# Value projection of 14 head groups by seven half-size products instead of eight (Strassen's scheme), with the last output product between its steps

## The chip, the cores and the metric

The kernel runs on one core of a Trainium2 chip. The core has five engines with queues of their own: TensorE (PE, matrix products, with a separate row PEld for its weight loads), VectorE (DVE), ScalarE (ACT), GpSimd (POOL) and SyncE (SP, which here only issues DMA). Each engine works its queue strictly in the order in which the program was written; between engines there are only semaphores. The metric is the time of one execution on the device in microseconds (us).

## The reference, cut to what matters

Two layers over `x` of shape 8 x 512 x 256, all in float32. Each layer normalises its input and adds an attention part and a feed-forward part to it. The change lies in the attention of the first layer, which has 16 heads of 64:

```
xn = layernorm(x)
q, k, v = xn @ Wq + bq, xn @ Wk + bk, xn @ Wv + bv        # each 256 -> 1024
q, k = rope(q), rope(k)
attended = softmax(causal(q k^T / 8)) @ v
x = x + attended @ Wo + bo + int8_product(xn)
```

The second layer (comparison attention and a gated feed-forward part) is not touched.

## The kernel before, in words

The work of layer 1 is cut into 16 groups, numbered `at` = 0 to 15. Group `at` is batch `b = at // 2` and half `g = at % 2` of the heads: eight heads, 512 of the 1024 columns of q, k and v. For each group the kernel does these steps:

- `project_qk` (line 428): queries and keys of the group, matrix products of 512 columns into PSUM, kept by ACT, and a rotated copy `y` fetched by DMA. `project(at, which)` calls it for both quarters of a group. `turn_qk` multiplies by the rotation's tables on DVE (line 446) and adds on POOL (line 461).
- `project_v` (line 472): the values of the group. For each of four tiles of 128 tokens, two accumulating products with 512 columns of `Wv` (the two halves of the 256 inputs), so eight products. ACT copies each bank to SBUF (line 478), and SP stores the result `v` to DRAM (line 479), from where `load_v` fetches it back rearranged as `vr` (line 489).
- `scores(at, run)` (line 509): query block times keys, in five runs that cover the 16 query blocks of 32 rows; run 3 is blocks 9, 5, 8 and 6, run 4 is block 7.
- `soften(at, run)`: DVE adds the mask and finds the maximum (line 537), ACT exponentiates and sums (line 541). `divide(at, run)`: DVE takes the reciprocal (line 552), POOL scales (line 560). `turn(at, run)`: DVE transposes 32 x 32 blocks into the tiles `t_0` to `t_3` (line 580).
- `weigh(at)` (line 597): chances times values into four banks. `keep_weighed`: ACT adds the bias (line 611).
- `output_product(at, half)` (line 390): attended times `Wo`, per half eight products of 256 columns. `add_output` (line 399): DVE adds it to the running output `x1`. `finish(at)` calls both for both halves.

The order is written out by hand in the loop `for at in range(1, last)` with `last = 15`; no scheduler moves anything. One iteration stands like this (DVE, ACT and POOL parts in brackets, in the order of their queues):

```
scores(at, 0)   [turn(at-1, 4); soften(at, 0)]
weigh(at-1)     [keep_weighed; turn_qk for the keys of at+1; divide(at, 0)]
scores(at, 1)   [soften; turn(at, 0); in some iterations look_at; divide(at, 1)]
project(at+1, 0)
scores(at, 2)   [soften; turn_qk for the queries of at+1; turn(at, 1); divide(at, 2);
                 prepare or turn_x of a later batch in some iterations]
project_v(at+1)
scores(at, 3)   [soften; turn_qk; turn(at, 2); divide(at, 3)]
scores(at, 4)   [soften]
                (at = 12 and 13: add_quantised)
finish(at-1)    [add_output x 2]
                [turn(at, 3)]
project(at+2, 1)
                [divide(at, 4); add_biases when g = 0]
```

`look_at` (statistics of a later batch's input) comes when g = 1, and `prepare` (normalising and its greatest value) too; `turn_x` comes when g = 0. Iteration `at = 1` also loads the constants of the rest, and on POOL it adds the biases to batch 0's output. Iteration `at = 14` leaves the loop after `project_v`; a tail written out by hand follows. PSUM has eight banks, which all these steps share.

Of the kernel before, what the change touches and what calls it, by code (L numbers as in the profile page):

```python
# [8 lines left out]
F32 = mybir.dt.float32  # L9
# [3 lines left out]
ALU = mybir.AluOpType  # L13
# [3 lines left out]
P = 128  # L17
B, S, D = 8, 512, 256
H, L = 16, 64
NT = S // P  # L20
NK = D // P
# [9 lines left out]
NH = NP // 4  # L31
# [13 lines left out]
def two_layers(  # L45
    ctx: ExitStack, tc, x, turns, Wq, Wk, Wv, Wo, w8, rows, sides, second, gates, out,
):
    nc = tc.nc
# [11 lines left out]
    def bank(name):  # L60
        return ps.tile([P, S], F32, tag="b", name=name)
# [23 lines left out]
    wqkv = [const.tile([P, NG, NK, 4 * L], F32, name=f"w{n}") for n in "qkv"]  # L85
# [49 lines left out]
    def load_second():  # L135
        nc.scalar.dma_start(crl, sides.rearrange("(k p) n -> p k n", p=P))
        nc.scalar.dma_start(gs, gates)
# [122 lines left out]
    with ExitStack() as c0:  # L260
        c0.enter_context(tc.manual_schedule())

        def pool(name, bufs, **kw):
            return c0.enter_context(tc.tile_pool(name=name, bufs=bufs, **kw))

        work = pool("work", 1)
# [3 lines left out]
        away = pool("away", 2, space=bass.MemoryType.DRAM)  # L270
# [20 lines left out]
        xnT = {}  # L291
# [71 lines left out]
        def scale_of_x():  # L363
            pb = bank("pmax")
            nc.tensor.transpose(pb[:, :P], spread.pop(0), ident)
            g = small.tile([P, 1], F32, tag="g", name="g", bufs=1)
            nc.vector.tensor_reduce(g, pb[:, :P], AX.X, ALU.max)
            nc.vector.tensor_scalar(xs[:, 0:1], g, 1.0 / 127.0, Q_EPS, ALU.mult, ALU.max)
            nc.vector.reciprocal(xs[:, 1:2], xs[:, 0:1])
# [4 lines left out]
        def fetch(b):  # L374
            x1s[b] = output_tile(f"x1_{b}")
            nc.sync.dma_start(x1s[b], tokens(b))
# [4 lines left out]

        products = {}

        def output_product(at, half):

            pw = bank(f"pw_{at}_{half}").rearrange("p (j n) -> p j n", j=2)
            for j in range(2):
                tok = bass.ts(2 * half + j, P)
                for p in range(4):
                    nc.tensor.matmul(  # L390
                        pw[:, j, :], atts[at, p][:, tok], wo[:, 4 * (at % NH) + p, :],
                        start=(p == 0), stop=(p == 3),
                    )
            products[at, half] = pw

        def add_output(at, half):
            b, g = divmod(at, NH)
            rows = slice(2 * half, 2 * half + 2)
            nc.vector.tensor_tensor(  # L399
                x1s[b][:, rows, :], products.pop((at, half)), x1s[b][:, rows, :], ALU.add  # L400
            )

            if g == NH - 1 and half == 1 and b < B - 1:
                nc.sync.dma_start(x1_far[b], x1s[b].rearrange("p t n -> p (t n)"))

        def finish(at):
            for half in range(2):
                output_product(at, half)
                add_output(at, half)
# [3 lines left out]
        evicted, stores = {}, {}  # L413
# [25 lines left out]
        def turn_qk(at, which):  # L439

            turn_own(at, which)
            turn_other(at, which)
# [20 lines left out]
        def project_v(at, halves=(0, 1)):  # L463
            b, g = divmod(at, NH)
            if 0 in halves:
                stores[at] = away.tile([4, P, NT * P], F32, tag="v", name=f"va_{at}")
            for half in halves:
                v = work.tile([P, 4, 2, P], F32, tag="v", name=f"v_{at}_{half}", bufs=2)
                for j in range(2):
                    pb = bank(f"pv_{at}_{half}_{j}")  # L470
                    for k in range(NK):
                        nc.tensor.matmul(  # L472
                            pb.rearrange("p (g n) -> p g n", g=2),
                            xnT[b][:, k, 2 * half + j],
                            wqkv[2][:, 2 * g : 2 * g + 2, k, :],
                            start=(k == 0), stop=(k == NK - 1),
                        )
                    nc.scalar.copy(v[:, :, j, :], pb.rearrange("p (r n) -> p r n", r=4))
                nc.sync.dma_start(
                    stores[at][:, :, half * 2 * P : half * 2 * P + 2 * P].rearrange("r p n -> p r n"),  # L480
                    v.rearrange("p r t n -> p r (t n)"),
                )

        def load_v(at):

            there = stores.pop(at)
            vs[at] = work.tile([P, 4, NT, P], F32, tag="vr", name=f"vr_{at}")
            for j in range(4):
                nc.sync.dma_start(
                    vs[at][j * Q : j * Q + Q].rearrange("p c t n -> p c (t n)"),  # L490
                    there[j].rearrange("(c k) n -> k c n", c=4),
                )
# [93 lines left out]
        half = S // Q // 2  # L586
# [192 lines left out]
        def project(at, which):  # L779
            for half in range(2):  # L780
                project_qk(2 * at + half, which)
# [60 lines left out]
        for at in range(1, last):  # L842
            b, g = divmod(at, NH)
            two = at + 2 <= last
            if g == 0 and b < B - 1:
                fetch(b)
            scores(at, 0)
            turn(at - 1, 4)
            soften(at, 0)
            if at == last - 3:  # L850
                scale_of_x()
            weigh(at - 1)
            keep_weighed(at - 1)
            if at == 1:
                load_rest()
                load_second()
                fetch(0)
            turn_qk(2 * at + 2, 1)
            load_v(at)
            if at in (last - 3, last - 2):  # L860
                s_ = at - last + 3
                fetch_output(s_, output_tile(f"x1e_{s_}"))
                xnl = fetch_input(s_, work.tile([P, NK * S], F32, tag="xnl", name=f"xnl_{s_}"))
            divide(at, 0)
            turn_qk(2 * at + 3, 1)
            if at == last - 2:
                first_norm = norm(0, xpool.tile([P, NT, D], F32, tag="x", name="yn_0"))
            scores(at, 1)
            soften(at, 1)
            turn(at, 0)  # L870
            if at == 2:
                look_at(2)
            elif at == 4:
                spread_rest()
                spread_second()
            elif g == 1 and 1 <= b < B - 2:
                look_at(b + 2)
            divide(at, 1)
            if at == last - 1:
                first_norm()  # L880
            project(at + 1, 0)
            if at in (last - 3, last - 2):
                round_input(xnl)
            scores(at, 2)
            soften(at, 2)
            turn_qk(2 * at + 2, 0)
            turn(at, 1)
            if at in (last - 3, last - 2):
                xq = work.tile([P, NK * S], BF16, tag="xq", name=f"xq_{s_}")
                clip(xnl, xq)  # L890
            divide(at, 2)
            if at == 2:
                prepare(2)
            elif g == 1 and 1 <= b < B - 2:
                prepare(b + 2)
            if g == 0 and 1 < b < B - 1:
                turn_x(b + 1)
                if b + 2 < B:
                    x_next.append(load_x(b + 2))
            if at == last - 1:  # L900
                turn_qk(2 * at + 3, 0)
            if at == 1:
                nc.gpsimd.tensor_tensor(bob, bob, rw[:, 2, :], ALU.add)
                add_biases(0)
            project_v(at + 1)
            if at == last - 1:
                break
            if at == 2:
                transpose_x(2)
                x_next.append(load_x(3))  # L910
            scores(at, 3)
            soften(at, 3)
            turn_qk(2 * at + 3, 0)
            turn(at, 2)
            divide(at, 3)
            scores(at, 4)
            soften(at, 4)
            if at in (last - 3, last - 2):
                for half in range(2):
                    add_quantised(s_, half, xq, line(f"u_{s_}_{half}"))  # L920
            finish(at - 1)
            turn(at, 3)
            if two:
                project(at + 2, 1)
            divide(at, 4)
            if g == 0 and b < B - 1:
                add_biases(b)
            if at == last - 4:
                greatest()


        at = last
# [52 lines left out]
        r = gate(0)  # L985
# [13 lines left out]
        for b in range(B):  # L999
# [18 lines left out]
            else:  # L1018
                r = gate(b)
# [17 lines left out]
            y = work.tile([P, NT, D], F32, tag="v", name=f"y_{b}", bufs=2)  # L1037
# [72 lines left out]
```

## Time and profile before

| | |
|---|---|
| median of 3 runs | 935.68 us (935.48 to 936.91) |
| span of the profiled execution | 934.3 us |
| PE busy | 919.8 us |
| DVE busy | 793.3 us |
| POOL busy | 542.2 us |
| ACT busy | 528.3 us |
| mean granted TensorE clock | 1.000 |

The profiled execution is one execution of its own; its own time is its span, from the first to the last instruction, 1.4 us under the median of the runs.

In the groups of the page, one program product in float32 appears as several records on PE (256 for the 128 products of `project_v`), so a cost is best taken from the timeline: where one group of instructions starts and where the next one does. A timeline row gives the start, the length, the engine and line, the operation, the output and input tiles with the shape of the first one, the count, and in brackets the idle time of the engine before it and what ended that.

### The profile page before, as it was taken

How to read it: one execution, taken by the hardware profiler on the slowest of the kernel's cores; microseconds unless marked ns; L12 is line 12 of the kernel's file. 1: busy time of each engine (PE TensorE's matmuls, PEld its weight loads, DVE VectorE, ACT ScalarE, POOL GpSimd, SP SyncE). 2: the span in 40 equal slices, each digit the busy share in tenths (PEclk: the TensorE clock that was granted, in tenths of full speed). 3: DMA queues.
4: the chain of work that ended last, by engine and by line, in shares of the span. 5: the costliest groups of instructions: out<-in, count | busy, mean ns of one | idle time of the engine just before them, and what ended most of it. 6: DMA issues, size and time to landing. Idle time of an engine off the chain costs nothing.

```text
span 934.3 us, 27432 instructions
## 1 busy us (share of the span) xinstructions
PE 919.8 (98%) x10451; PEld 594.7 (64%) x10451; DVE 793.3 (85%) x2441; ACT 528.3 (57%) x1478; POOL 542.2 (58%) x688
## 2 busy tenths in 40 slices
PE   9998999999999999999999999999999999999998
PEld 5446565656566575757565656566657777777776
DVE  4998898898899889988998899999899588888854
ACT  3585564647465646474746556555577444445553
POOL 2576766655665667566665756678667323444311
PEclk9999999999999999999999999999999999999999
DMA  7667354525543464245444635563435133221011
GB/s 213 194 165 213 102 138 130 121 75 132 169 105 97 109 182 132 75 115 172 123 95 114 179 93 145 151 154 97 110 108 127 47 102 79 74 50 48 25 33 34
DMA packets 70290, 108.03 MB, mean 116 GB/s; under 512 B 8592, under 2 KB 49040, under 8 KB 70160
## 3 DMA queue, kind: packets, MB, share of 16 engines
q1 hardware_dynamic: 68288, 104.64, 42.2%
q10 hardware_dynamic: 1872, 1.64, 0.7%
q8 instruction: 83, 1.36, 0.6%
q14 instruction: 47, 0.39, 0.1%
HBM read 41.76 MB, written 28.84 MB: 76 GB/s over the span
## 4 chain that ended last, share of the span: by engine, by line
PE 85%; DVE 6%; DMA 3%; issue 1%; POOL 1%; SPq 1%; ACT 1%; DVEq 0%; ACTq 0%; POOLq 0%
PE pq L428 21%; PE av L597 14%; PE sc L509 11%; PE pw L390 10%; PE pv L472 8%; PE po L756 6%; PE pk L703 3%; PE pg L718 3%; PE pvv L730 3%; DVE t L580 2%; PE c L675 2%; PE trc L743 1%; PE plr L245 1%; DVE p L537 1%; DMA xnl<-xnf 1%
## 5 line engine op out<-in xcount | busy, mean ns | idle before, releaser
L541 ACT ACTIVATE p<-p,nm 128x64 f32<-128x64 f32 (+15 forms) x512 | 260.0, 512 | 123.8 <-DVE nm L537 100.9
L560 POOL TENSOR_SCALAR p<-p,rs 128x512 f32<-128x512 f32 (+4 forms) x504 | 265.4, 547 | 44.6 <-DVE rs L552 42.6
L461 POOL TENSOR_TENSOR h<-h,y 128x1024 f32<-128x1024 f32 x62 | 161.1, 2598 | 181.5 <-DVE y L446 102.2
L537 DVE CUSTOM_DVE_ANT_0 p<-sc,cmask 128x64 f32<-128x64 f32 (+15 forms) x512 | 190.2, 434 | 53.7 <-PE sc L509 53.7
L580 DVE STREAM_TRANSPOSE t<-p 128x256 f32<-128x256 f32 (+3 forms) x640 | 192.2, 367 | 17.9 <-POOL p L560 17.8
L509 PE MATMUL sc<-h,h 64*32 64x512 f32 (+15 forms) x4096 | 138.7, 393 | 1.3 <-POOL h L461 1.2
L597 PE MATMUL av<-t,vr 32*64 32x384 f32 (+15 forms) x4096 | 128.8, 392 | 3.7 <-issue 3.7
L597 PEld LDWEIGHTS av<-t,vr 32*64 32x64 f32 x4096 | 122.8, 131 | 9.2 <-issue 7.9
L509 PEld LDWEIGHTS sc<-h,h 64*32 64x32 f32 x4096 | 78.6, 106 | 78.5 <-issue 58.3
L434 ACT ACTIVATE l<-pq,cs 128x512 f32<-128x512 f32 x128 | 84.7, 683 | 67.6 <-PE pq L428 53.3
L390 PE MATMUL pw<-wo,att 128*128 128x256 f32 x512 | 114.9, 382 | 0.8 <-DVE nm L537 0.8
L446 DVE TENSOR_TENSOR y<-y,cs 128x1024 f32<-128x1024 f32 x64 | 110.6, 1728 | 5.1 <-DMA y<-l 5.1
L428 PE MATMUL pq<-xnT,wq 128*128 128x512 f32 x256 | 114.6, 599 | 0.2 <-ACT xnT L349 0.2
L428 PE MATMUL pq<-xnT,wk 128*128 128x512 f32 x256 | 113.1, 593 | 1.4 <-DVE x L399 1.0
L472 PE MATMUL pv<-wv,xnT 128*128 128x512 f32 x256 | 114.3, 599 | 0.0
L390 PEld LDWEIGHTS pw<-wo,att 128*128 128x128 f32 x512 | 95.9, 190 | 19.5 <-issue 6.1
L541 ACT ACTIVATION_READ_ACCUMULATOR p<-p,nm 128x1 f32 x512 | 97.3, 190 | 0.0
L428 PEld LDWEIGHTS pq<-xnT,wk 128*128 128x128 f32 x256 | 48.3, 190 | 58.2 <-issue 55.4
L472 PEld LDWEIGHTS pv<-wv,xnT 128*128 128x128 f32 x256 | 47.3, 190 | 57.9 <-issue 54.5
L446 DVE TENSOR_TENSOR h<-l,cs 128x1024 f32<-128x1024 f32 x64 | 80.0, 1252 | 4.3 <-ACT l L434 4.3
L428 PEld LDWEIGHTS pq<-xnT,wq 128*128 128x128 f32 x256 | 47.2, 190 | 56.0 <-issue 48.8
L611 ACT ACTIVATE att<-av,cs 128x512 f32<-128x512 f32 x64 | 38.7, 688 | 71.3 <-PE av L597 71.3
(114 smaller groups left out, 940.7 us busy)
## 6 DMA issues: line engine op xcount, KB each, us to landing
y<-l SPq DMA_DIRECT2D x256, 128.0 KB, 2.3
va<-v SPq DMA_DIRECT2D x32, 512.0 KB, 3.1
vr<-va SPq DMA_DIRECT2D x64, 256.0 KB, 5.1
x<-in_x SPq DMA_DIRECT2D x15, 512.0 KB, 5.0
x1f<-x SPq DMA_DIRECT2D x7, 512.0 KB, 3.2
out<-y SPq DMA_DIRECT2D x14, 256.0 KB, 2.2
xnf<-xs SPq DMA_DIRECT2D x5, 512.0 KB, 3.6
xnT<-xnf SPq DMA_DIRECT2D x20, 128.0 KB, 2.8
```

The lines of the kernel that those rows point to most:

```text
L390: nc.tensor.matmul(pw[:, j, :], atts[at, p][:, tok], wo[:, 4 * (at % NH) + p, :], start=(p == 0), stop=(p == 3),)
L428: nc.tensor.matmul(pb.rearrange("p (t a r) -> p t a r", a=4, r=Q), w[:, g, k, bass.ts(t, P)], xnT[b][:, k].rearrange("p a (t r) -> p t a r ...
L434: nc.scalar.activation(l[:, t, :], pb, AF.Identity, bias=cs[:, bias : bias + 1])
L446: nc.vector.tensor_tensor(dst, src, table[:, None, :].to_broadcast([P, 2, S]), ALU.mult)
L461: (engine or nc.gpsimd).tensor_tensor(h, h, y, ALU.add)
L472: nc.tensor.matmul(pb.rearrange("p (g n) -> p g n", g=2), xnT[b][:, k, 2 * half + j], wqkv[2][:, 2 * g : 2 * g + 2, k, :], start=(k == 0), ...
L509: nc.tensor.matmul(scored[at, i][e][j * Q : j * Q + Q, :], q[rows, j % 2, bass.ts(i, Q)], k[rows, j % 2, :n], start=True, stop=True,)
L537: nc.vector.tensor_tensor_reduce(p[:, e, col : col + n], sc, cmask[:, S - n :], -1.0 / L**0.5, BIG, ALU.add, ALU.min, nm[:, c : c + 1],)
L541: nc.scalar.activation(p[:, e, col : col + n], p[:, e, col : col + n], AF.Exp, bias=nm[:, c : c + 1], scale=-1.0, accum_out=sm[:, c : c + 1],)
L560: nc.gpsimd.tensor_scalar(p, p, rs[:, c : c + 1], 1.0, ALU.mult, ALU.mult)
L580: nc.vector.transpose(turned[at][c][:, :, at_ : at_ + (n - 1) * pitch(c) + 1 : pitch(c), :], p[:, :, c * P : c * P + n * Q].rearrange("p e ...
L597: nc.tensor.matmul(banks[j][e * L : e * L + L, i * Q :], vs[at][rows, c, m, bass.ts(e, L)], t[c][rows, e, m * pitch(c) + m : m * pitch(c) ...
```

## The change

The values of groups 2 to 15 are computed by a scheme of seven products in place of eight (Winograd's form of Strassen's). The group's 512 tokens, 256 inputs and 512 columns are each cut into halves; each product takes a 128-input block for 256 tokens and 256 columns, and so is two matmuls of 256 columns.

- `sum_weights` forms three sums of the blocks of `Wv` for both halves of the heads, and overwrites one block with a fourth, once, on POOL, in iteration at = 1. `mix_input` forms four differences of a batch's input blocks on POOL, when g = 1.
- `project_v_by_seven` runs the seven products in three banks. Bank x takes four of them one on top of the other; ACT copies it out after each (`keep`), so the next product waits for the copy. Bank z takes two. DVE adds y once and z twice to the copies (`add`). The second product of z waits for z's first add.
- `output_product(at-1, 0)` now stands before the seven products, and the two quarters of `output_product(at-1, 1)` between them; `finish(at-1)` after `scores(at, 4)` is gone. In iteration at = 14 nothing stands between.
- The two stores of `v` come after the last copy and after the last add.
- The program is built with a smaller scratch area for DMA descriptors, which makes room for the new tiles.

```diff
-        def output_product(at, half):
-            pw = bank(f"pw_{at}_{half}").rearrange("p (j n) -> p j n", j=2)
-            for j in range(2):
+        def output_product(at, half, js=(0, 1)):
+            if 0 in js:
+                products[at, half] = bank(f"pw_{at}_{half}").rearrange("p (j n) -> p j n", j=2)
+            pw = products[at, half]
+            for j in js:
...
+        def sum_weights():
+            one, two, three = (wv_sums[:, :, n] for n in range(3))
+            (a11, a12), (a21, a22) = ([wv[:, :, h, k] for k in range(NK)] for h in range(2))
+            for dst, x, y, op in (
+                (one, a21, a22, ALU.add), (two, one, a11, ALU.subtract),
+                (a21, a11, a21, ALU.subtract), (three, a12, two, ALU.subtract),
+            ):
+                nc.gpsimd.tensor_tensor(dst, x, y, op)
...
+        def mix_input(b):
+            t = work.tile([P, 4, 2, P], F32, tag="tx", name=f"tx_{b}")
+            (b11, b12), (b21, b22) = ([xnT[b][:, k, 2 * h : 2 * h + 2] for h in range(2)] for k in range(NK))
+            for dst, x, y in ((0, b12, b11), (1, b22, t[:, 0]), (2, b22, b12), (3, b21, t[:, 1])):
+                nc.gpsimd.tensor_tensor(t[:, dst], x, y, ALU.subtract)
+            mixes[b] = t
+
+        def project_v_by_seven(at, fillers=(None, None), between=lambda: None):
...
+            def product(to, left, right, fresh=False):
+                for j in range(2):
+                    nc.tensor.matmul(
+                        to[:, j, :], left[:, j], right, start=fresh and j == 0, stop=True,
+                        skip_group_check=j > 0 or not fresh,
+                    )
...
+            def keep(half, g_):
+                nc.scalar.copy(part(half, g_), of(x))
+
+            def add(bank_, half, g_):
+                nc.vector.tensor_tensor(part(half, g_), of(bank_), part(half, g_), ALU.add)
...
+            product(x, b11, a11, True)
+            keep(0, 0)
+            product(y, b21, a12, True)
+            product(z, t1, s1, True)
+            product(x, t2, s2)
+            keep(1, 0)
+            add(y, 0, 0)
+            if fillers[0]:
+                fillers[0]()
+            product(x, t3, s3)
+            keep(1, 1)
+            if fillers[1]:
+                fillers[1]()
+            add(z, 1, 1)
+            product(x, t4, a22)
+            keep(0, 1)
+            store(0)
+            between()
+            product(z, b22, s4)
+            add(z, 1, 0)
+            store(1)
...
             project(at + 1, 0)
+            if at == 1:
+                sum_weights()
+            if g == 1:
+                mix_input(b + 1)
...
-            project_v(at + 1)
             if at == last - 1:
+                project_v_by_seven(at + 1)
                 break
+            output_product(at - 1, 0)
+            add_output(at - 1, 0)
+            project_v_by_seven(
+                at + 1, [lambda j=j: output_product(at - 1, 1, (j,)) for j in range(2)],
+                lambda: add_output(at - 1, 1),
+            )
...
-            finish(at - 1)
             turn(at, 3)
```

More of the change, by code (lines that the diff above doesn't have):

```diff
@@ L393, in output_product @@
                     )
-            products[at, half] = pw
         def add_output(at, half):
@@ L482, in project_v @@
                 )
+        wv = wqkv[2].rearrange("p (g h) k n -> p g h k n", h=2)
+        wv_sums = work.tile([P, 2, 3, 2 * P], F32, name="wv_sums")
+        def sum_weights():
[6 more added lines that the diff above has]
+                nc.gpsimd.tensor_tensor(dst, x, y, op)
@@ new lines, in two_layers, with part, of, store @@
+        mixes = {}
+        def mix_input(b):
[5 more added lines that the diff above has]
+        def project_v_by_seven(at, fillers=(None, None), between=lambda: None):
+            b, g = divmod(at, NH)
+            stores[at] = away.tile([4, P, NT * P], F32, tag="v", name=f"va_{at}")
+            s1, s2, s4 = (wv_sums[:, g, n] for n in range(3))
+            (a11, a12), (s3, a22) = ([wv[:, g, h, k] for k in range(NK)] for h in range(2))
+            t1, t2, t3, t4 = (mixes[b][:, n] for n in range(4))
+            b11, b21, b22 = xnT[b][:, 0, 0:2], xnT[b][:, 1, 0:2], xnT[b][:, 1, 2:4]
+            x, y, z = (bank(f"pv_{at}_{n}").rearrange("p (j n) -> p j n", j=2) for n in range(3))
+            v = [work.tile([P, 4, 2, P], F32, tag="v", name=f"v_{at}_{half}", bufs=2) for half in range(2)]
+            def product(to, left, right, fresh=False):
[4 more added lines that the diff above has]
+                    )
+            def part(half, g_):
+                return v[half][:, 2 * g_ : 2 * g_ + 2].rearrange("p r j n -> p j r n")
+            def of(bank_):
+                return bank_.rearrange("p j (r n) -> p j r n", r=2)
+            def keep(half, g_):
+                nc.scalar.copy(part(half, g_), of(x))
+            def add(bank_, half, g_):
+                nc.vector.tensor_tensor(part(half, g_), of(bank_), part(half, g_), ALU.add)
+            def store(half):
+                nc.sync.dma_start(
+                    stores[at][:, :, half * 2 * P : half * 2 * P + 2 * P].rearrange("r p n -> p r n"),
+                    v[half].rearrange("p r t n -> p r (t n)"),
+                )
[20 more added lines that the diff above has]
+            store(1)
@@ L904, in two_layers @@
                 add_biases(0)
-            project_v(at + 1)
             if at == last - 1:
+                project_v_by_seven(at + 1)
                 break
+            output_product(at - 1, 0)
[3 more added lines that the diff above has]
+                lambda: add_output(at - 1, 1),
+            )
             if at == 2:
@@ L1095 @@
     from concourse.bass_utils import run_bass_kernel_spmd
-    nc = bacc.Bacc("TRN2", target_bir_lowering=False, num_devices=1)
+    nc = bacc.Bacc(
+        "TRN2", target_bir_lowering=False, num_devices=1, dynamic_dma_scratch_size=1024
+    )
     arrays, args = {}, []
```

## The prediction

> **What bounds the kernel now.** The page's busy table and its chain of waits come first.
>
> ```profile
> span 934.3 us, 27432 instructions
> PE 919.8 (98%) x10451; PEld 594.7 (64%) x10451; DVE 793.3 (85%) x2441; ACT 528.3 (57%) x1478; POOL 542.2 (58%) x688
> ...
> PE 85%; DVE 6%; DMA 3%; issue 1%; POOL 1%; SPq 1%; ACT 1%; DVEq 0%; ACTq 0%; POOLq 0%
> ```
>
> PE is busy 98% of the span and 85% of the chain: time leaves only by shortening PE's list, and any hole in it adds time. VectorE (DVE) is at 85%, so the question is how late it may be. I read this from one iteration of the loop, at = 6, in the timelines: PE first (start, length, what).
>
> ```profile
> 317.53 2.01 PE L509 MATMUL sc<-h,h 64*32 64x384 f32 x64
> 319.47 7.13 PE L472 MATMUL pv<-wv,xnT 128*128 128x512 f32 x16
> 326.53 2.39 PE L509 MATMUL sc<-h,h 64*32 64x320 f32 x80
> 328.85 7.17 PE L390 MATMUL pw<-wo,att 128*128 128x256 f32 x32
> 335.86 7.08 PE L428 MATMUL pq<-xnT,wk 128*128 128x512 f32 x16
> 342.87 1.96 PE L509 MATMUL sc<-h,h 64*32 64x512 f32 x48
> 344.75 5.64 PE L597 MATMUL av<-t,vr 32*64 32x512 f32 x159
> ```
>
> No hole: value projection (pv), last scores, output product (pw), next keys (pq), next scores, then weigh (av). A clean iteration lasts 44.24 us (weigh to weigh, 344.75 to 388.99). DVE and POOL in the same stretch:
>
> ```profile
> 327.83 0.45 DVE L537 CUSTOM_DVE_ANT_0 p<-sc,cmask 128x320 f32<-128x320 f32 x1
> ...
> 335.53 0.20 DVE L552 RECIPROCAL rs<-sm 128x4 f32<-128x4 f32 x2
> ...
> 336.31 1.28 DVE L399 TENSOR_TENSOR x<-pw,x 128x512 f32<-128x512 f32 x2
> 337.51 2.83 DVE L580 STREAM_TRANSPOSE t<-p 128x256 f32<-128x256 f32 x10
> 340.27 0.12 DVE L552 RECIPROCAL rs<-sm 128x2 f32<-128x2 f32 x1
> 341.45 0.77 DVE L580 STREAM_TRANSPOSE t<-p 128x256 f32<-128x256 f32 x2 [1.06 <-POOL p L560]
> ```
>
> ```profile
> 335.77 3.65 POOL L560 TENSOR_SCALAR p<-p,rs 128x320 f32<-128x320 f32 x8 [0.42 <-DVE rs L552]
> 340.49 0.93 POOL L560 TENSOR_SCALAR p<-p,rs 128x256 f32<-128x256 f32 x2 [1.07 <-DVE rs L552]
> ```
>
> From the last scores to weigh runs a second chain: soften(at,3), the rotation, turn(at,2), divide on POOL, turn(at,3), divide, turn(at,4). Weigh's first matmul reads all 16 query blocks of t_0, so it needs the first transpose of turn(at,4): done at 341.84 here, with weigh at 344.75. That slack of 2.9 us is there because pw and pq, 14 us of PE work, stand between scores and weigh. The change takes pw away from there.
>
> **Part 1, PE's list.** pv starts 7.06 us before the next group: 8 products of 0.883. pw takes 7.01 for 16 products of 256 columns: 0.438 each, weight loads hidden. Fourteen such take 6.13, so each of 14 groups saves 0.93: **-13.0**. Products that accumulate are among pw's, so I take no other price.
>
> **Part 2, weigh waits.** In the new order pw stands before and between the seven products. From the start of scores(at,3) PE needs 2.32 + 7.01 (pq) + 1.88 (scores) = 11.2 us to weigh (before: 18.2). The chain needs: 1.1 until the first two score banks are full (0.96 of matmuls; scores of 2.12 us were answered after 1.2); 7.8 from the first softening to the second reciprocal (327.83 to 335.65); divide(at,3) on POOL ends at 11.6 (339.42); then about 0.6 for the last two transposes and 0.1 for the reciprocal, 0.1 to POOL, 0.93 of divide, 0.4 for the first transpose: 13.75. That the two adds of pw (1.2) leave this stretch shortens it by only 0.25, since turn(at,3) then runs into POOL. With 0.1 of signalling: 15.0. DVE can't begin earlier, because its queue holds the three adds of the seven just before, the last of which waits for the last product, itself just before scores(at,3); that add (0.64, by L399, one PSUM and one SBUF operand as here) fits into the 1.1. So weigh starts 15.0 - 11.2 = 3.8 late, in the 13 iterations at = 1 to 13: **+48.8** (13 x 3.75). Bounds: if POOL and DVE interleave better, 2.5; if the last add takes twice 0.64, 4.3. Nothing gives it back: scores, weigh, pq, pw, the seven follow on PE in order, and the chain starts again from the next scores.
>
> **Part 3, waits inside the seven.** In plain iterations none: from scores(at,2) = 0, x is copied by ACT at 6.4 to 7.0 (softening ends at 5.8) and needed again at 8.1; both later copies lie beside 1.75 us of pw; z's add ends near 12.9 and the last product wants it at 14.2. ACT copies as often as before (4 of 0.58).
> Where it fails:
> - at = 1, from POOL's timeline: POOL ends divide(1,1) at 92.0, then sums the weights (4 of 512 columns, 1.25 each by L218's 2.50 for two) and mixes x (4 of 0.70, by L380's 2.79 for four), ahead of the rotation's add (2.37), divide (3.65 at best) and the biases (0.72 + 1.4 for the first half). With 2.2 us lost to DVE's two rotation products that is 110.3. add_output(0,0) on DVE now stands ahead of z's add and waits for those biases; z's add ends at 112.3, the last product was due at 104.8: **+7.5** (4 to 10).
> - at = 14 has no output product between: x's copies come bare. x2 waits for ACT's softening (6.45 instead of 4.6), x3 and x4 for 0.8 each: **+3.4**.
> - at = 3, 5, 7, 9, 11: prepare (3.2 us of DVE) stands ahead of the adds, z's add ends at 14.3 against 14.2. The mixes add a conflict: POOL's and DVE's two-operand instructions exclude each other (DVE 305.32 took 3.38 where 302.92 took 1.22, while POOL's add took 3.33 instead of 2.37). POOL, 2.8 late, now has its add (2.37) beside the normalising. Each 0 to 3.1, I take 1.5: **+7.5**.
>
> [...]
>
> **Part 4, rest.** Holes of before that a later PE no longer meets (iterations over 44.24: 1.1 at the transposes of at = 2, 1.85 at 4, 0.7 at 6, 0.3 at 8, 1.45 at 10, 0.8 at 12): **-6.2**. At 12 and 13 POOL has two adds (2.5) between the divides, which lengthens the chain by 1.75 while the quantised products give PE 0.9 more: **+1.7**. Stores of v go out up to 2 us later on SP, ahead of the loads of y; load_v comes 15 us after, so nothing. Fetched xnT lands 18.3 after scores(at,2), pq now wants it at 17.4: 0.9, inside weigh's wait. The scratch size touches no queue in use.
>
> **Sum.** -13.0 + 48.8 + 7.5 + 3.4 + 7.5 - 6.2 + 1.7 = +49.7. The profiled span is 934.3; the median of the runs is 935.68, 1.4 around it. 935.7 + 49.7 = **985**.
>
> **Clock.** The longest hole of before, 70.3 to 72.5, left the granted clock at 1.00 in the next 3.5 us. Mine are 3.8. [...] I take 0 from the row; the high end: if half of weigh (8.05) ran at half speed after each hole, 13 x 4 = 52.
>
> **Rivals.**
> - *Milder gate*, 967: weigh is 2.5 late (13 x 1.25 = 16 less). For it: DVE and POOL overlap pieces more finely than I sum. 18%.
> [...]
> - *No saving* on PE: if a half product took 0.504 instead of 0.438, part 1 is zero and the time 998. Against it: 512 of them in L390 at 0.449 busy. 3%, within the forecast's spread.
> - *Faster*, 922: DVE's lag. If DVE's and POOL's chain from scores(at,3) to turn(at,4) took 11.2 or less, every new wait fell into DVE's idle time (7.2 us in iteration 6: 0.93, 3.42, 1.06, 1.82) and only -13.0 stayed. It decides at weigh; the rows give 15.0, so 5%.
> - *No change*, 936: a chain of 12.2 would wait 1.0 per iteration against the 0.93 saved. 4%.
>
> **How the numbers follow.** Forecast 985 (970 to 1000) 60%, with no saving in it; milder 18%, harsher 13%, faster 5%, same 4%. Slower by over 0.2% (about what a measurement tells from no change): 0.91. The range 958 to 1006 takes in the milder gate, the bounds of parts 2 and 3 and the first of the harsher cases.
>
> **What would show it.** PE with a hole of 3.5 to 4 us before every weigh, ended by DVE's transpose; weigh to weigh near 47 us; 14 half products in 6.1 us; a hole of several us at at = 1 before the last product. Wrong if weigh starts 11.2 us after scores(at,3) without a hole, or if holes sit inside the seven in plain iterations.

## The result, and the profile after

The changed kernel takes 1019.72 us (median of 4 runs, 1019.09 to 1020.14); beside it on the same chip the kernel before took 936.29. The ratio is 1.089, with a 95% interval of 1.0875 to 1.0906. The change makes the kernel slower by 8.9%. The forecast of 985 has the sign right and the size wrong, and 1020 lies above the range of 958 to 1006. Of all executions reported below one stands apart: the profiled one of the kernel best1 took 2447 us, with TensorE busy 2.6 times as long as in the next profile of the same kernel, and best1's median and ratio leave it out.

The profiled execution spans 1017.9 us, 83.6 more than that of before. Its page, in the busy table, the row of the granted clock over 40 slices, and the chain of waits:

```profile
span 1017.9 us, 27834 instructions
...
PE 937.6 (92%) x10619; PEld 643.5 (63%) x10619; DVE 834.4 (82%) x2483; ACT 526.2 (52%) x1478; POOL 574.8 (56%) x720
...
PEclk9999989898999998999999999999999999999999
...
PE 66%; DVE 18%; POOL 5%; issue 4%; ACT 3%; DMA 2%; SPq 1%; DVEq 0%; ACTq 0%; POOLq 0%
```

Three things are to be seen. PE's share fell from 98% to 92%: there are holes now. DVE's share of the chain went from 6% to 18% and POOL's from 1% to 5%: those are what the holes wait for. And PE is busy for 937.6 us instead of 919.8, although its list is shorter by some 13 us: part of what is left runs slower. The clock, 1.000 on average before, is 0.965.

Where the holes are, PE's timeline of the iteration at = 6 shows (start, length, operation, first shape, count, and in brackets the idle time before it and what ended that):

```profile
355.30 3.72 PE L392 MATMUL pw<-wo,att 128*128 128x256 f32 x16
358.86 1.89 PE L518 MATMUL pv<-wv,xnT 128*128 128x256 f32 x8
360.58 1.89 PE L518 MATMUL pv<-wv_sums,tx 128*128 128x256 f32 x8
...
367.49 1.03 PE L518 MATMUL pv<-wv_sums,xnT 128*128 128x256 f32 x4
368.45 2.39 PE L588 MATMUL sc<-h,h 64*32 64x320 f32 x80
370.90 7.11 PE L429 MATMUL pq<-xnT,wk 128*128 128x512 f32 x16
377.93 1.96 PE L588 MATMUL sc<-h,h 64*32 64x512 f32 x48
383.72 10.57 PE L676 MATMUL av<-t,vr 32*64 32x512 f32 x256 [3.83 <-DVE t L659]
```

Output product and seven products take 13.15 us together (355.30 to 368.45); before, value projection and output product took 14.09 (363.75 to 370.82 and 373.13 to 380.15 in the kernel before). The saving is there: 0.94. But weigh starts 15.27 after scores(at, 3), where PE's own work is 11.4, and then it lasts 10.50 instead of 7.95. DVE and POOL in the same stretch tell why it starts late:

```profile
377.37 0.20 DVE L631 RECIPROCAL rs<-sm 128x4 f32<-128x4 f32 x2
...
378.69 1.48 DVE L659 STREAM_TRANSPOSE t<-p 128x256 f32<-128x256 f32 x5 [0.45 <-POOL p L639]
...
380.46 1.56 DVE L659 STREAM_TRANSPOSE t<-p 128x256 f32<-128x256 f32 x5 [0.28 <-POOL p L639]
381.94 0.12 DVE L631 RECIPROCAL rs<-sm 128x2 f32<-128x2 f32 x1
383.13 0.77 DVE L659 STREAM_TRANSPOSE t<-p 128x256 f32<-128x256 f32 x2 [1.06 <-POOL p L639]
```

```profile
377.61 3.67 POOL L639 TENSOR_SCALAR p<-p,rs 128x320 f32<-128x320 f32 x8 [0.42 <-DVE rs L631]
382.16 0.94 POOL L639 TENSOR_SCALAR p<-p,rs 128x256 f32<-128x256 f32 x2 [0.88 <-DVE rs L631]
```

This is the chain of part 2, link by link: reciprocal, divide(at, 3), the transposes that follow it piece by piece, the last reciprocal, divide(at, 4), and the first transpose of turn(at, 4), 383.13, which lets weigh go. In all 13 iterations weigh starts 0.05 to 0.15 after the end of that transpose, also where the profile names "issue" as what ended the hole. The view by stretches tells why weigh lasts longer (stretch, its length, busy time of PE, PEld, DVE, ACT and POOL, then the granted clock, the share of DMA, GB/s):

```profile
376.00:379.80 3.80, 3.80 (x53) 1.37 (x51) 3.35 (x16) 1.81 (x6) 3.38 (x6) 1.00 0.08 28
379.80:383.60 3.80, 0.09 (x20) 0.00 (x0) 2.45 (x10) 1.58 (x3) 2.92 (x7) 0.86 0.54 122
383.60:388.00 4.40, 4.28 (x56) 3.50 (x64) 4.40 (x15) 3.41 (x12) 2.24 (x4) 0.50 0.61 139
388.00:389.50 1.50, 1.50 (x40) 1.42 (x32) 1.50 (x4) 0.07 (x1) 0.61 (x1) 0.54 0.00 0
389.50:394.20 4.70, 4.70 (x181) 4.68 (x164) 3.81 (x2) 0.00 (x0) 4.70 (x3) 1.00 0.01 3
...
431.70:435.60 3.90, 0.03 (x6) 0.01 (x1) 2.55 (x10) 1.63 (x3) 2.46 (x6) 1.00 0.45 103
435.60:440.00 4.40, 4.38 (x127) 4.40 (x135) 4.40 (x15) 3.46 (x12) 0.00 (x0) 1.00 0.76 171
```

In the hole from 379.8 to 383.6 the clock falls to 0.86, the first 4.4 us of weigh run at 0.50 (56 records where the same stretch of the next iteration has 127), and only at 389.5 is it 1.00 again. One iteration later a hole just as long leaves the clock at 1.00, and weigh takes 7.98. Of the 13 weighs behind the new holes two took 7.98, three 9.4 to 9.6, eight 10.1 to 10.7.

### The profile page after: what moved, and what is told of

Read it like the earlier page. It is cut to its first block, busy times and chain, and to the rows that moved or that the text cites. A ratio compares the mean times of both kernels' runs of the same rounds, so it can differ in the third digit from the quotient of the medians.

```text
span 1017.9 us, 27834 instructions
## 1 busy us (share of the span) xinstructions
PE 937.6 (92%) x10619; PEld 643.5 (63%) x10619; DVE 834.4 (82%) x2483; ACT 526.2 (52%) x1478; POOL 574.8 (56%) x720
## 3 DMA queue, kind: packets, MB, share of 16 engines
q8 instruction: 84, 1.38, 0.6%
## 4 chain that ended last, share of the span: by engine, by line
PE 66%; DVE 18%; POOL 5%; issue 4%; ACT 3%; DMA 2%; SPq 1%; DVEq 0%; ACTq 0%; POOLq 0%
PE av L676 15%; PE pq L429 11%; PE sc L588 8%; PE pw L392 7%; DVE t L659 6%; PE po L835 5%; PE pv L518 5%; DVE p L616 4%; POOL p L639 3%; PE pk L782 3%; PE pg L797 3%; PE pvv L809 3%; DVE y L447 3%; DVE h L447 2%; ACT l L435 2%
## 5 line engine op out<-in xcount | busy, mean ns | idle before, releaser
L639 POOL TENSOR_SCALAR p<-p,rs 128x512 f32<-128x512 f32 (+4 forms) x504 | 262.0, 542 | 48.5 <-DVE rs L631 47.2
L659 DVE STREAM_TRANSPOSE t<-p 128x256 f32<-128x256 f32 (+3 forms) x640 | 194.3, 368 | 25.4 <-POOL p L639 25.3
L676 PE MATMUL av<-t,vr 32*64 32x96 f32 (+15 forms) x4096 | 154.0, 450 | 48.5 <-issue 25.7
L676 PEld LDWEIGHTS av<-t,vr 32*64 32x64 f32 x4096 | 139.7, 148 | 63.2 <-issue 50.8
L392 PE MATMUL pw<-wo,att 128*128 128x256 f32 x512 | 119.3, 382 | 0.0
L447 DVE TENSOR_TENSOR y<-y,cs 128x1024 f32<-128x1024 f32 x64 | 113.1, 1767 | 6.3 <-DMA y<-l 6.3
L435 ACT ACTIVATE l<-pq,cs 128x512 f32<-128x512 f32 x128 | 80.8, 680 | 25.4 <-PE pq L429 23.0
L530 ACT COPY v<-pv 128x512 f32<-128x512 f32 x56 | 32.8, 586 | 93.1 <-PE pv L518 93.1
L767 ACT ACTIVATE e<-c,nb 128x512 f32<-128x512 f32 x32 | 21.7, 683 | 72.5 <-DVE nb L762 72.0
```

Source lines behind the costliest of these rows:

```text
L392: nc.tensor.matmul(pw[:, j, :], atts[at, p][:, tok], wo[:, 4 * (at % NH) + p, :], start=(p == 0), stop=(p == 3),)
L435: nc.scalar.activation(l[:, t, :], pb, AF.Identity, bias=cs[:, bias : bias + 1])
L447: nc.vector.tensor_tensor(dst, src, table[:, None, :].to_broadcast([P, 2, S]), ALU.mult)
L639: nc.gpsimd.tensor_scalar(p, p, rs[:, c : c + 1], 1.0, ALU.mult, ALU.mult)
L659: nc.vector.transpose(turned[at][c][:, :, at_ : at_ + (n - 1) * pitch(c) + 1 : pitch(c), :], p[:, :, c * P : c * P + n * Q].rearrange("p e ...
L676: nc.tensor.matmul(banks[j][e * L : e * L + L, i * Q :], vs[at][rows, c, m, bass.ts(e, L)], t[c][rows, e, m * pitch(c) + m : m * pitch(c) ...
```

## The experiments

At this point the theory is that the moved output product opens a hole of 3.8 us before each weigh, as forecast, and behind most of these holes weigh begins at half clock, for 3 to 6 us. There are two rivals: weigh is slower for another reason (its operands, DMA traffic), or the seven products themselves are what costs.

**Filling the hole with products that nobody reads.** Before each weigh of groups 1 to 13, PE gets four (warm4) or two (warm2) products of 512 columns into a bank that weigh then overwrites; the output stays as it is.

```diff
             banks = [bank(f"av_{at}_{j}") for j in range(4)]
+            for _ in range(4 if 1 <= at < last - 1 else 0):
+                nc.tensor.matmul(banks[0], ident, cmask, start=True, stop=True)
```

> Four matrix products of 512 columns that nobody reads stand before each of the 13 late weighs (groups 1 to 13), so that PE works through 3.5 of the 3.9 us in which it waits. Theory (the wait is set by DVE and POOL, and the empty wait costs TensorE its clock afterwards): weigh starts as late as in the changed kernel, but lasts 8.0 us each time instead of 8.0 to 10.7, about 24 us less: 993 to 998, granted clock 0.99 or more. Rival (weigh is slow for another reason, its values or its weight loads): 1020 or a little more, weigh as long as now.

> The same with two such products, 1.8 us of work, so that 2.1 us of empty wait are left. [...] If holes near 2.3 us can already cost the clock, as the first weigh of the changed kernel suggests (9.38 us after 2.33 us), between 1000 and 1010. Rival (not the clock): 1020.

Measured: warm4 takes 1003.65 us (ratio 1.0706, 1.0674 to 1.0737), clock 0.993; warm2 1005.22 (1.0718, 1.0682 to 1.0754), clock 0.982. warm2 lies in its expected range, warm4 above its 993 to 998: two stretches at half clock are left in it, behind the other waits at at = 1 and at = 14 (after a hole of 5.03 us and the bare copies, rows of 2.07 and 2.08 for work whose row is 1.03 elsewhere). A kernel with more work for PE is faster than the one without, by 1.7% of the time. PE's timeline of warm4, same iteration:

```profile
369.38 3.70 PE L672 MATMUL av<-cmask,ident 128*128 128x512 f32 x8
373.01 7.87 PE L678 MATMUL av<-t,vr 32*64 32x512 f32 x256
```

The dead products take the hole's place and weigh is back at 7.80 (11 of the 13 between 7.8 and 8.2). So neither its operands nor the DMA traffic made it slow, since both are the same here; the idle of PE did. warm2, two iterations:

```profile
322.58 1.98 PE L672 MATMUL av<-cmask,ident 128*128 128x512 f32 x4
326.47 9.67 PE L678 MATMUL av<-t,vr 32*64 32x512 f32 x256 [1.90 <-DVE t L659]
...
371.65 1.98 PE L672 MATMUL av<-cmask,ident 128*128 128x512 f32 x4
375.44 8.04 PE L678 MATMUL av<-t,vr 32*64 32x512 f32 x256 [1.80 <-DVE t L659]
```

Half the hole is left, and it still costs: four weighs behind holes of 1.90 and 1.91 us and one behind 2.45 took 9.5 to 9.7, while those behind 1.91 (twice), 1.80, 2.11 and the shorter ones took 8.0. A hole half as long loses less often and less each time (1.6 to 1.7 us), but of these eight holes of 1.90 to 2.45 us five cost and three didn't.

**The move alone.** The eight products stay; only the output product goes to where the change puts it, one half ahead of the projection and one behind.

```diff
+            output_product(at - 1, 0)
+            add_output(at - 1, 0)
             project_v(at + 1)
...
+            output_product(at - 1, 1)
+            add_output(at - 1, 1)
...
-            finish(at - 1)
```

> The kernel before with eight products as they were, but the output product of the group before moved: its first half ahead of the value projection, its second half right behind it. Theory (what the output product covered is DVE's and POOL's chain from the last scores to weigh): a hole of some 4 us before each of 13 weighs and a slower clock after most of them, 50 us plus some 25: 1005 to 1015. Rival (the waits come from the seven products themselves, the move is free): 936.

Measured: 1009.63 us (ratio 1.0769, 1.0739 to 1.0798), clock 0.968, with holes of 3.8 to 4.4 before the weighs of groups 1 to 13 (at = 11 apart, where another small product cuts the hole in two) and weighs of 9.3 to 10.9. This is what I expected. One of them:

```profile
369.46 1.96 PE L509 MATMUL sc<-h,h 64*32 64x512 f32 x48
375.18 9.69 PE L597 MATMUL av<-t,vr 32*64 32x512 f32 x256 [3.77 <-DVE t L580]
```

Without any of the seven products the kernel loses 7.7% of the 8.9%: the place of the output product costs most. So in this order the rival falls, that the scheme itself is what costs.

**The seven products alone.** The scheme as in the change, without the fillers, and `finish(at - 1)` back behind `scores(at, 4)`.

> The seven products without anything between them, the output product left where it was. Theory: no hole before weigh; instead the copies of bank x and the adds of bank z hold PE inside the seven, as at = 14 of the changed kernel shows (1.62 + 0.68 + 0.68 + 1.53 us), more where prepare stands ahead of the adds: 3.7 to 6.7 us per iteration, 985 to 1015. Rival (the move alone costs, the seven are a gain): 923 to 930.

Measured: 1028.57 us (ratio 1.0965, 1.094 to 1.099). That is above what I expected, and slower than the change itself. No hole is left before weigh, as expected, but the holes have moved into the seven:

```profile
316.20 2.08 PE L518 MATMUL pv<-wv_sums,xnT 128*128 128x256 f32 x4 [3.96 <-DVE v L533]
...
361.77 1.13 PE L518 MATMUL pv<-wv_sums,tx 128*128 128x256 f32 x4 [1.61 <-ACT v L530]
363.57 1.13 PE L518 MATMUL pv<-wv,tx 128*128 128x256 f32 x4 [0.68 <-ACT v L530]
365.38 1.13 PE L518 MATMUL pv<-wv,tx 128*128 128x256 f32 x4 [0.68 <-ACT v L530]
366.96 1.13 PE L518 MATMUL pv<-wv_sums,xnT 128*128 128x256 f32 x4 [0.45 <-DVE v L533]
```

Bare, bank x waits for each of ACT's copies and z for its add, 3.4 us together in a plain iteration. In odd iterations z's second product waits longer for its first add, which stands behind `prepare`, up to 3.96, and here it then runs at a lower clock (0.65 from 316.2 to 322.0; a row of 2.08, for work whose row is 1.03 at full clock). So the scheme needs fillers, and the chain to weigh needs the same work as cover: the whole of pw can't be in both places.

**Half of it in each place.** In best1 only the first half of the output product fills the gaps, in pieces of 4, 2 and 2 products; the second stays behind `scores(at, 4)`. The weights' sums are made before the loop, the mixes and normalising go to where POOL is free, `divide(at, 4)` ahead of `turn(at, 3)`, and the turning of the next input between z's two adds. order1 is the same order with the eight products.

> The seven products keep only half an output product between them (four, two and two of its eight products ahead of the second, third and fourth product of x, which is what the copies of x take); the other half stays behind the last scores. The reciprocal and divide of run 4 go ahead of turn(at,3), so POOL divides without a break; the weights are summed ahead of the loop, the inputs are mixed ahead of scores(at,1), normalising a later batch goes to POOL, and its greatest value and turn_x go where DVE waits. Theory: from the last scores PE needs 14.7 us to weigh and the chain 14.4, so there is no hole and no lost clock, x and z wait nowhere, and an iteration takes 43.3 to 43.9 us instead of 44.2: 920 to 932. Rival (the seven cost DVE and POOL more than PE wins, wherever they stand): 936 or more, with holes at weigh.

> The same order and moves with the eight products of before, so without sums, mixes and adds. It tells what of the gain is the order's: only the waits that single iterations of before had can go, some 5 us: 929 to 934. If the seven products bring 0.93 us per group, best1 is 8 to 13 us under this; rival: this one is the faster.

> The version with half an output product between the seven once more, for a profile: the first one fell on an execution with a TensorE 2.6 times slower than all others. Its four other times were 963.7 to 969.7, so a profile of 962 to 968 with clock near 0.99 is expected. If the chain from the last scores to weigh still decides, there are holes at weigh; if the seven's own waits decide, they stand ahead of x's and z's products.

Both missed: best1 967.0 us (ratio 1.0315, 1.0292 to 1.0338), order1 944.25 (1.0074, 1.006 to 1.0088). best1b is the same kernel as best1 once more (964.9, one execution). Its trace has at most 0.84 us of hole before the weighs of groups 1 to 12, but a new one ahead of the keys in the even iterations:

```profile
335.03 3.72 PE L391 MATMUL pw<-wo,att 128*128 128x256 f32 x16
342.42 8.80 PE L428 MATMUL pq<-xnT,wk 128*128 128x512 f32 x16 [3.67 <-DMA xnT<-xnf]
```

I had turned the next input later and projected its keys earlier, and the fetch of `xnT` did not land in time: 2.9 to 4.5 us in four even iterations and 0.8 in a fifth, 15 in all, and in two of them the projection itself took longer as well (8.7 instead of 7.0). order1 has the same fault, smaller.

**The same with those waits removed.** best2 turns the next input before `project(at + 1, 0)`, puts the normalising at the end of the odd iterations, and moves four smaller things its expectation names; best3 also takes the store of the turned input out of the way of the loads of y. order2 and order3 are the same orders with eight products.

```diff
             divide(at, 1)
+            if g == 0 and 1 < b < B - 1:
+                greatest_of(b + 1)
+                if at < last - 3:
+                    turn_x(b + 1)
...
             project(at + 1, 0)
...
+            elif g == 0 and 1 < b < B - 1:
+                fetch_turned(b + 1)
...
+                    lambda n=n: output_product(at - 1, 0, n)
+                    for n in (range(4), *((range(4, 6), range(6, 8)) if at < last - 1 else ((), ())))
...
             soften(at, 4)
...
+            add_output(at - 1, 0)
+            output_product(at - 1, 1)
+            add_output(at - 1, 1)
+            divide(at, 4)
...
             turn(at, 3)
```

> best1 with the waits taken away that its profile shows. The store and transposes of the next input go ahead of project(at+1, 0) and its fetch behind it (project(at+2, 1) waited for that fetch: 14.9 us in five iterations, and ran 1.7 longer at half clock in two of them); normalising goes to the end of the odd iterations on POOL and its greatest value to the next iteration (0.74 before weigh in five odd iterations, and weigh 0.5 to 1.0 longer there); the clip of at = 12 and 13 and the last rotation of at = 14 go behind the adds (z waited 0.69, 2.03 and 1.53); POOL's adds behind divide (1.14); one half of the last half product goes back to the tail (weigh waited 1.91 there and ran 2.2 longer). These sum to about 33 off a span of 962.8. Theory (the seven products save 0.93 of PE per group and cost nothing more where no hole is left before weigh or inside them): span about 930, median 927 to 935, ratio 0.990 to 0.999. Rival (VectorE's three adds per group, 2.0 us, keep the chain to weigh late wherever they stand, so that new holes take the place of the old): 940 or more, with holes ended by VectorE.

> The same order as best2 with the eight products of before in place of the seven (no sums, no mixes, no adds). Theory: 13 us more of PE than best2 but less for VectorE and POOL, so about 940 (934 to 945), slower than best2 by 5 to 13. Rival (the seven pay nothing in any order): best2 at or above order2.

> best2 with the store of the turned input issued behind the loads of y on SP instead of ahead of them. In best2 VectorE waits 1.74 and 1.94 us for y behind that store at 231.71 and 498.79, and z's last product then 1.09, 0.38 and 1.29 in three even iterations. Theory (those holes are only the queue's): they go, span about 929.7, median about 931 (929.5 to 932.5). Rival (they come from VectorE's added work, greatest value and transposes in that iteration): no change, 933.9.

> order2 (eight products) with the same store moved. It had no hole there, so nothing should change: 934.1, span 929.8. If the seven products are worth in this order what their rows differ by (a plain iteration of best2 is 43.91, of order2 44.24, over 13 iterations about 4 us, less 1.4 where x's copies come bare at at = 14), best3 is 2 to 4 below order3; if they are worth the 0.93 a group that the rows of before give, 10 or more below.

| kernel | products | median us | ratio to before (95%) | a plain iteration |
|---|---|---|---|---|
| best2 | seven | 933.86 | 0.9968 (0.9958 to 0.9978) | 43.91 |
| order2 | eight | 934.11 | 0.9968 (0.9955 to 0.9981) | 44.24 |
| best3 | seven | 932.13 | 0.9954 (0.9941 to 0.9968) | 43.72 to 43.95 |
| order3 | eight | 934.07 | 0.9982 (0.9969 to 0.9994) | 44.24 |

best2 came out as expected; in best3 z's holes in the even iterations are gone, so they were the queue's, and it beats both kernels: 0.5% under the one before and 8.6% under the change. But order2 came out at the low end of its expectation and equal to best2, where I had expected 5 to 13 us between them. best3 and order3 differ by 1.9 us, with intervals that just fail to overlap. Some 1.4 of this may be the clock (an estimate: its mean over the executions is 0.9984 in best3 and 0.9969 in order3, of 933 us), so no run here shows clearly that the seven products are worth anything in the whole. The 13 us that 14 groups save by the rows of the change aren't there. The timelines of a plain iteration show where part of them went, best3's for PE and then for ACT, and order3's for PE:

```profile
403.54 1.99 PE L531 MATMUL pv<-wv,xnT 128*128 128x256 f32 x8
...
412.60 1.03 PE L531 MATMUL pv<-wv_sums,xnT 128*128 128x256 f32 x4
413.55 2.39 PE L600 MATMUL sc<-h,h 64*32 64x320 f32 x80
```

```profile
407.40 0.56 ACT L543 COPY v<-pv 128x512 f32<-128x512 f32 x1
409.19 0.59 ACT L543 COPY v<-pv 128x512 f32<-128x512 f32 x1 [1.22 <-PE pv L531]
410.99 0.59 ACT L543 COPY v<-pv 128x512 f32<-128x512 f32 x1 [1.22 <-PE pv L531]
412.80 0.59 ACT L543 COPY v<-pv 128x512 f32<-128x512 f32 x1 [1.22 <-PE pv L531]
```

```profile
404.81 7.13 PE L486 MATMUL pv<-wv,xnT 128*128 128x512 f32 x16
...
415.33 2.39 PE L600 MATMUL sc<-h,h 64*32 64x320 f32 x80
```

The seven and their eight fillers take 10.01; the eight products and the same fillers take 10.52 in order3 (404.81 to 415.33). So the saving is 0.51 and not 0.94. With a filler of only two products between them, bank x is a loop of its own: product, signal, copy, signal, 1.80 from copy to copy, where PE has 1.72 of work (0.86 for the product and 0.86 for the filler, by the rows of the change). Three such turns are some 0.3 of the 0.43 that is missing. Single iterations of best3 lose more: z waits 0.79 at at = 1, a run of scores 0.78 at at = 6, xnT is 1.65 late at at = 12, and at at = 14 x waits twice for 0.68 and the next scores 1.46 for a rotation (order3 has one wait of 2.93 there). I didn't follow these further.

## Why the prediction was wrong

Term by term, from the holes of the two PE timelines (those over 0.2 us) and the lengths of weigh:

| step of the prediction | forecast | measured in the trace |
|---|---|---|
| PE's list (14 groups) | -13.0 | -13.2 (0.94 each) |
| weigh waits, 13 iterations | +48.8, and 1.7 at 12 and 13 | +48.9 in all |
| at = 1 | +7.5 | 2.48 + 5.06 = 7.5 |
| at = 3, 5, 7, 9, 11 | +7.5 | 1.71 + 1.73 + 1.71 + 1.78 + 1.71 = 8.6 |
| at = 14 | +3.4 | 1.62 + 0.68 + 0.68 + 1.53 = 4.5 |
| old holes | -6.2 | -5.7 |
| keys that wait ahead of weigh (three, 0.3 to 1.4) | none | +2.2 |
| clock | 0 | +29, and 1.5 that I can't place |

**The step that failed is Clock: "I take 0 from the row."** Without it the terms give +53 against the forecast's +50. The 14 weighs take 25.9 us more than 7.95 each, and four groups behind the holes at at = 1 and at = 14 another 3.4, 29 together. The row it was taken from was true and decided nothing. It is the first hole, of 2.3 us, ahead of the first weigh; here it is in the view by stretches, in the kernel before and then in the changed one:

```profile
70.30:72.50 2.20, 0.00 (x0) 0.01 (x1) 2.20 (x9) 0.11 (x1) 0.61 (x2) 1.00 0.99 306
72.50:76.00 3.50, 3.48 (x95) 3.50 (x103) 3.50 (x14) 2.57 (x7) 0.00 (x0) 1.00 0.67 159
```

```profile
69.90:72.20 2.30, 0.00 (x1) 0.00 (x1) 2.30 (x10) 0.21 (x1) 0.73 (x2) 0.94 0.98 303
72.20:74.00 1.80, 1.77 (x18) 1.37 (x26) 1.80 (x6) 0.86 (x3) 0.00 (x0) 0.50 0.97 216
```

The same hole left the clock at 1.00 in the one execution and halved it for some 3 us in the other. Over the kernels of this study the first weigh took 7.98 to 8.11 after it in six profiles and 9.4 to 9.6 in six others. The changed kernel, warm2 and warm4 are the same program up to there, and of these three only warm4 went free. So one row is one draw. A sum over 13 holes needed a chance and a price for each: what the changed kernel shows is 11 of 13, with 2.2 us on average. My high end, 52, rested on weigh's first half at half speed after each hole; somewhat over half of that is what came.

What decides the draw no run shows: none moved a hole on purpose. Two holes of the changed kernel, 3.83 and 3.89 us long, went different ways. Here are stretches of 3.4 us around the one and the other:

```profile
379.15:382.55 3.40, 0.74 (x32) 0.31 (x16) 2.63 (x10) 2.23 (x4) 2.52 (x6) 1.00 0.33 75
382.57:385.96 3.39, 2.24 (x24) 1.84 (x32) 2.83 (x9) 1.37 (x4) 3.27 (x6) 0.50 0.91 207
385.98:389.38 3.40, 3.40 (x71) 2.94 (x63) 3.40 (x11) 2.10 (x10) 0.49 (x1) 0.50 0.14 34
...
430.35:433.75 3.40, 1.38 (x48) 0.50 (x30) 2.83 (x10) 2.98 (x8) 2.88 (x7) 1.00 0.05 13
433.77:437.16 3.39, 1.54 (x29) 1.57 (x37) 2.32 (x9) 0.62 (x1) 0.94 (x2) 1.00 0.89 204
```

Around the first, PE is busy for 0.74 us of one stretch, and the clock is 0.50 in the two behind it (1.00 again from 389.5). Around the second, PE is busy for 1.38 and 1.54 us, and the clock is 1.00 in both. Two cases give no rule. With 11 of 13 and 2.2 us, a new hole cost 1.9 us on average in this kernel beside its length; the first hole, 1.5 us in six profiles of twelve, some 0.8 (both estimates from these counts).

The other steps held. The chain of 15.0 from scores(at, 3) to weigh was 15.27 in the iteration above. It is as long where the hole is smaller (2.47 at at = 4, 3.42 at at = 8): there PE had already waited 1.44 and 0.47 ahead of the keys. At at = 1 the last product waited, as forecast, for an add that stands behind the biases. PE lost the first 2.48 of the 7.5 earlier, on the mixes, which I had not seen; the sum came out because the biases set when the second wait ends. On DVE:

```profile
110.88 0.69 DVE L400 TENSOR_TENSOR x<-pw,x 128x512 f32<-128x512 f32 x1 [8.05 <-POOL x L380]
```

At at = 14 I had x's waits and not z's, of 1.53 for its add. In the five odd iterations DVE's normalising took 2.50 to 3.93 where it took 1.95 before. In each of them one of its four instructions began while POOL's add of 2.4 ran, and ended 0.14 to 0.16 after it: at at = 3 the add ran from 210.58 to 212.94 and the instruction from 211.47 to 213.09, 1.62 instead of 0.38. What DVE lost follows what was left of the add when the instruction began: 1.24 of 1.47 us here, 0.55 of 0.78 at at = 5, 2.06 of 2.29 at at = 9. The five iterations lost 1.71 to 1.78 each; the 3.1 at the top of my range is shown by no run, and the 1.5 that I took was near. Two slips in the prediction's numbers change nothing: the milder rival is 969 by its own sum and not 967, and the 512 of L390 are records, two to a product. The case that came nearest is the harsher one, given 13%; the row that misled is what spoke against it.

## What to carry to other kernels

Work that stands between two steps of a chain on other engines is cover, and moving it costs the cover wherever the chain is longer than what remains: price the chain and the cover before the saving. A hole on TensorE can cost more than its length: here holes of 1.90 us and longer were followed by a lower clock in some cases and not in others; in 14 places of the changed kernel it stood at half for 3.4 or 6.8 us. Count it with a chance and a price, taken from the traces of the kernel, and never as zero because one hole in one execution went unpunished. And a scheme that trades products for copies and adds is worth what is left after its own loop through PSUM: here 0.3 to 0.5 us in a plain iteration, of the 0.94 that the list promised, and less than that over the whole kernel.

## What the runs showed of the hardware that I had not expected

- Idle PE of 1.90 us was followed by a clock of 0.60 over the next 3.6 us (warm2, 326.4 to 330.0), 1.80 us in another iteration by 1.00.
- After a hole of 3.8 us the clock was 0.50 from 382.57 to 389.38 (the changed kernel), though PE was busy from 383.72 on.
- Products that nobody reads made the kernel faster by 1.7% (warm4, ratio 1.0706 against 1.089).
- POOL took 6.4 to 6.7 us for the normalising of four 128x256 tiles (6.43 and 6.44 in best1b, 6.69 and 6.70 in best2) that DVE does in 1.95 alone (the kernel before).
